# Row sums for a Winograd convolution: two 64-row products, one per half of the columns, in place of one product with a block diagonal table

## The chip, the cores and the metric

The kernel runs on one core of one Trainium2 chip. The metric is the device time of one execution in microseconds. Three runs of the kernel before took 3293.95, 3282.76 and 3287.43 us; the median is 3287.43 us. One further execution was profiled; it took 3285.59 us, and the first to the last instruction in its trace, the span, is 3283.7 us.

## The reference

The input is a batch of 32 images of 56 x 56 places with 96 channels, in float32. Layer 0 is a convolution block, layer 1 a block with a Fourier transform along the tokens and a quantised feed-forward part. Cut to what is computed:

```python
# layer 0
h  = (x - mean(x)) * rsqrt(var(x) + 1e-5) * ln_w + ln_b          # over the 96 channels
x1 = (h @ w_in + b_in)[..., :192]
y  = conv3x3(x1, conv_w, padding="SAME") + conv_b                # 192 -> 96 channels
x  = x + silu(y)
# layer 1, t is x as (32, 3136, 96)
n  = layernorm(t)
h  = relu(bn(n @ w1.T))                                          # 192 channels
X  = fft(h, axis=tokens, norm="ortho")
xr = relu(X.real * rd - X.imag * idg + rb); xi = relu(X.imag * rd + X.real * idg + ib)
t  = t + bn(ifft(xr + 1j * xi).real @ w2.T)
t  = t + quantised_ffn(layernorm(t))                             # 96 -> 384 -> 96
```

The input transform of the convolution is the place of the change. The 3x3 convolution is done as a one-dimensional Winograd scheme along the rows of an image: four output rows come from six sums of input rows, so each of the 14 groups of four rows needs six weighted sums of the rows around it.

## The kernel before

**Layout.** A token of an image is row r and column c of 56 x 56. With `N1 = 112` partitions and `N2 = 28` columns per partition, partition 2r + h holds the 28 columns of half h of row r. All token stages work on tiles of 112 partitions.

**The stage that changes.** An image comes in four chunks of columns, `LN_CHUNKS` (8, 8, 8 and 4 of the 28). `fetch` (L335) loads a chunk `xl` from the input by a DMA on SP's queue. `take_in` (L343) calls `stats` (L120), which takes the sums over the channels on VectorE, the variance on VectorE (L131) and its power of -1/2 on GpSimd (L133), and then scales the chunk on VectorE into one of two buffers `xa` (L349), whose 97th channel is a constant one. `make_image` (L351) calls `image` (L144), which does one TensorE product for each column place j of a chunk. The stationary operand is `xa[:, j, :]`, 112 rows by 97 channels, and the moving one is the table `rows6_sb`, 112 rows by 168 columns. The table has 2 x 6 x 14 columns: for each half h, each of the six sums k and each of the 14 groups g. Since partition 2r + h belongs to half h, an entry is other than zero only where the row's half is the column's half; this is the block diagonal table. So one product yields for 97 channels all 84 sums of both halves. Up to three products share one PSUM tile of tag `q`, and one ScalarE copy (L149) puts them into the image buffer `img`.

**What follows.** `conv` (L151) multiplies `img` with the transformed weights `wv` in 18 products per chunk, on PSUM tiles of the same tag `q`, which has two buffers of one bank each. `to_tokens` (L188) transposes the result, again on tag `q`. The Fourier stages, the products with `w1` and `w2` and the feed-forward part follow with PSUM tiles of other tags.

**Products in float32.** Each float32 product shows as two weight loads and two matmuls in the trace[...]. 28 places x 32 images are 896 products of L148 and 1792 records of each kind.

**Order of the work.** `plan` gives every step of every image a place on a time axis of eight units per image, `order.sort` merges the images, and `run` issues the steps in that order. So the convolution of an image stands beside the Fourier part of the image before it. The program is then put in its final order on each engine by a scheduler that works on an estimated timeline, so neighbouring instructions on TensorE come from several stages. In `plan`, `make_image` stands at up to three places for each chunk, three column places at a time (L500 to L504): 11 steps per image.

## Time and profile before

| | |
|---|---|
| median of three runs | 3287.43 us |
| profiled execution, its own time | 3285.59 us |
| its span, first to last instruction | 3283.7 us |
| TensorE matmul records busy | 3201.2 us, 97% of the span |
| TensorE weight loads busy | 2821.3 us, 86% |
| VectorE busy | 2711.9 us, 83% |
| ScalarE busy | 2319.2 us, 71% |
| GpSimd busy | 586.2 us, 18% |
| mean granted TensorE clock | 0.989 |
| image products (L148) | 1792 matmul records, 324.0 us busy, 308 ns each |
| their copies (L149) | 352, 182.2 us busy in three shapes |
| mean DMA traffic | 108 GB/s |

Busy time of an engine is the time in which at least one of its records runs. [...]the next record may begin before it ends. So the duration of a matmul record is a latency. What a record costs TensorE in a dense stream is the distance from its start to the next start. The trace's timeline merges neighbouring records of one kind into a row with a start and a count; the start of the next row less that of this row, divided by the count, is that distance.

### The profile page before, as it was taken

To read this page: it belongs to the slowest core of one execution; us is meant where nothing else is said; L and a number is where in the kernel's file an instruction comes from. 1 tells how busy PE (TensorE), PEld (TensorE's weight loads), DVE (VectorE), ACT (ScalarE), POOL (GpSimd) and SP (SyncE) were. 2 spreads that over 40 slices of the span, in tenths; PEclk is the share of its full clock that TensorE was granted. 3 is DMA by queue.
4 is the path that set the end of the run, shared out by engine and by line. 5 is a ranking of instruction groups with operands and counts; after the bars stand their busy time and mean duration, and the time that the engine had idled before them with its cause. 6 is when DMAs were issued, how large, how long until landed. Compare 5 with 4: busy or idle time off the path is not lost. (4 is left out here: it accounts for less than half of the span.)

```text
span 3283.7 us, 69648 instructions
## 1 busy us (share of the span) xinstructions
PE 3201.2 (97%) x24597; PEld 2821.3 (86%) x24597; DVE 2711.9 (83%) x8306; ACT 2319.2 (71%) x5616; POOL 586.2 (18%) x397
## 2 busy tenths in 40 slices
PE   6999999999999999999999999999999999999987
PEld 5888888888888888888888888888888888888875
DVE  5568888888888888888888888888888888887887
ACT  2567777777777777777777776777777777777676
POOL 2111112111112111112111112111112111111111
PEclk9999999999999999999999999999999999999997
DMA  4343344433344433344433344433344333443331
GB/s 109 102 110 104 96 114 121 118 105 108 92 121 123 118 102 106 98 119 121 117 106 100 104 121 117 118 97 103 107 121 123 106 108 94 116 121 104 98 108 55
DMA packets 330839, 355.61 MB, mean 108 GB/s; under 512 B 125577, under 2 KB 283673, under 8 KB 330265
## 3 DMA queue, kind: packets, MB, share of 16 engines
q1 hardware_dynamic: 328482, 348.99, 38.5%
q8 instruction: 195, 3.19, 0.4%
q10 hardware_dynamic: 2008, 2.17, 0.2%
q14 instruction: 154, 1.25, 0.1%
HBM read 196.92 MB, written 154.14 MB: 107 GB/s over the span
## 5 line engine op out<-in xcount | busy, mean ns | idle before, releaser
L159 PE MATMUL cv<-img,wv 97*96 97x224 f32 (+1 forms) x4608 | 863.8, 330 | 6.2 <-DVE wv L607 5.4
L159 PEld LDWEIGHTS cv<-img,wv 97*96 97x96 f32 x4608 | 675.1, 163 | 88.1 <-issue 7.1
L133 POOL TENSOR_TENSOR rs_c<-var_c,mhalf 112x8 f32<-112x8 f32 (+1 forms) x128 | 194.1, 1517 | 1900.5 <-DVE var_a L131 994.0
L222 PEld LDWEIGHTS px<-fb_sb,at 112*96 112x96 f32 x3584 | 399.7, 164 | 87.7 <-issue 30.6
L222 PE MATMUL px<-fb_sb,at 112*96 112x112 f32 (+1 forms) x3584 | 429.8, 261 | 20.6 <-DMA at<-da 17.4
L254 PEld LDWEIGHTS pg<-w2a,gt 96*112 96x112 f32 (+1 forms) x3584 | 394.2, 179 | 33.4 <-DVE gt L246 2.9
L254 PE MATMUL pg<-w2a,gt 96*112 96x96 f32 (+1 forms) x3584 | 403.9, 262 | 1.4 <-DVE gt L246 0.6
L226 ACT ACTIVATE av<-px,par_sb 96x224 f32<-96x224 f32 (+1 forms) x448 | 200.1, 447 | 267.8 <-PE px L222 263.4
L284 ACT CAST h<-pf 128x448 f16<-128x448 f32 x672 | 362.5, 539 | 25.2 <-PE pf L282 22.2
L204 PE MATMUL ph<-w1a,n2t 97*112 97x192 f32 x1792 | 369.0, 328 | 1.5 <-ACT n2t L197 1.2
L213 PE MATMUL pa<-h,fa_sb 112*112 112x384 f32 x896 | 366.3, 491 | 0.1
L207 ACT ACTIVATE h<-ph,rs_b 112x192 f32<-112x192 f32 x896 | 330.3, 426 | 29.3 <-PE ph L204 27.9
L148 PE MATMUL im<-rows_sb,xa 112*97 112x168 f32 x1792 | 324.0, 308 | 11.3 <-DVE xa L349 9.6
L133 POOL TENSOR_TENSOR rs_b<-var_b,mhalf 112x8 f32<-112x8 f32 (+1 forms) x128 | 191.7, 1498 | 748.1 <-DVE var_b L131 423.9
L204 PEld LDWEIGHTS ph<-w1a,n2t 97*112 97x112 f32 x1792 | 286.8, 177 | 39.5 <-ACT n2t L197 1.8
L292 DVE TENSOR_SCALAR h<-h,b1q 128x448 f16<-128x448 f16 x658 | 214.2, 326 | 112.0 <-ACT h L284 110.7
L459 DVE TENSOR_SCALAR xn<-t,st_c,rs_c 112x96 f32<-112x96 f32 x896 | 240.0, 320 | 75.4 <-POOL rs_c L133 75.3
L148 PEld LDWEIGHTS im<-rows_sb,xa 112*97 112x97 f32 x1792 | 263.9, 165 | 35.0 <-issue 10.3
L214 ACT COPY u<-pa 112x384 f32<-112x384 f32 x448 | 216.5, 483 | 101.3 <-PE pa L213 97.4
L293 DVE CAST hq<-h 128x448 fp8e5<-128x448 f16 x672 | 257.2, 383 | 12.7 <-ACT h L290 5.9
L237 DVE SCALAR_TENSOR_TENSOR sv<-px,par_sb,av 96x224 f32<-96x224 f32 (+1 forms) x448 | 197.4, 441 | 70.9 <-ACT av L228 66.1
L282 PE MATMUL pf<-n3t,w1q 96*128 96x448 fp8e5 x672 | 242.2, 360 | 8.8 <-ACT h L284 7.6
(110 smaller groups left out, 6022.9 us busy)
## 6 DMA issues: line engine op xcount, KB each, us to landing
da<-u SPq DMA_DIRECT2D x224, 336.0 KB, 3.2
at<-da SPq DMA_DIRECT2D x224, 336.0 KB, 3.8
de<-es SPq DMA_DIRECT2D x224, 168.0 KB, 2.3
y<-de SPq DMA_DIRECT2D x224, 168.0 KB, 2.8
out<-o SPq DMA_DIRECT2D x224, 168.0 KB, 2.2
xl<-in_x SPq DMA_DIRECT2D x96, 336.0 KB, 3.9
x<-in_x SPq DMA_DIRECT2D x96, 336.0 KB, 3.2
xl<-in_x SPq DMA_DIRECT2D x32, 168.0 KB, 2.3
```

The source lines that it names most:

```text
L133: nc.gpsimd.tensor_tensor(rs, var, mhalf[:, :n], ALU.pow)
L148: nc.tensor.matmul(ps[:, j], xa[:, j, :], rows6_sb, start=True, stop=True)
L159: nc.tensor.matmul(ps[:, at], wv[:, k, dx, :], cols, start=(dx == 0), stop=(dx == 2))
L204: nc.tensor.matmul(ph[:, j, :], n2t[:, 2 * j2 + j, :], w1a, start=True, stop=True)
L207: nc.scalar.activation(h[:, j], ph[:, j], AF.Relu, scale=rs[:, 2 * j2 + j : 2 * j2 + j + 1])
L213: nc.tensor.matmul(pa, fa_sb, h, start=True, stop=True)
L222: nc.tensor.matmul(px[:, j], at[:, j, i * C : (i + 1) * C], fb_sb[:, first(p) : first(p + 1)], start=True, stop=True)
L254: nc.tensor.matmul(pg[:, j, :], lhs, w2a[:, i, :], start=(i == 0), stop=(i == 1))
L282: nc.tensor.matmul(pf, w1q[:, k * 128 : (k + 1) * 128], n3t, start=True, stop=True)
L284: nc.scalar.copy(h1, pf)
L293: nc.vector.tensor_copy(hq[:, k, :], h2, saturate=False)
L459: nc.vector.tensor_scalar(xc[:, j], im.t[i][:, at, :C], mu[:, at : at + 1], rs[:, at : at + 1], ALU.subtract, ALU.mult)
```

## The change

The image stage takes its input from a second copy of the input, `xh`, laid out in advance by the host program: for each image, 128 rows of 28 columns, of which rows 0 to 55 are the left halves of the image rows, rows 64 to 119 are the right halves, and rows 56 to 63 and 120 to 127 are zeros. `fetch` loads 128 partitions of it. `stats`, the scaling and the buffers `xa` have 128 partitions in this stage; the rest of the kernel keeps 112.

The table `rows6_sb` has the 84 sums once for partitions 0 to 63 and once for 64 to 127. `image` does two products for each column place: rows 0 to 63 with the left half, rows 64 to 127 with the right half, each with a moving operand of 64 rows by 84 columns. The products of the two halves go to two PSUM tiles of tag `q`, up to four column places in each, and two ScalarE copies put them into `img`. `plan` has seven steps of four column places per image where it had 11 of up to three.

```diff
     def image(xa, n, b, j0):
-        ps = psq.tile([C + 1, n, 2, WC * WG], F32, tag="q", name=f"im_{b}_{j0}")
+        ps = [psq.tile([C + 1, n, WC * WG], F32, tag="q", name=f"im_{b}_{j0}_{h}") for h in range(2)]
         for j in range(n):
-            nc.tensor.matmul(ps[:, j], xa[:, j, :], rows6_sb, start=True, stop=True)
-        nc.scalar.copy(img[:, :, j0 + 1 : j0 + 1 + n].rearrange("c h j k g -> c j h (k g)"), ps)
+            for h in range(2):
+                rows = slice(64 * h, 64 * h + 64)
+                nc.tensor.matmul(ps[h][:, j], xa[rows, j, :], rows6_sb[rows], start=True, stop=True)
+        for h in range(2):
+            nc.scalar.copy(img[:, h, j0 + 1 : j0 + 1 + n].rearrange("c j k g -> c j (k g)"), ps[h])
...
-    rows6_sb = const.tile([N1, 2 * WC * WG], F32, name="rows6_sb")
+    rows6_sb = const.tile([128, WC * WG], F32, name="rows6_sb")
-    xas = [const.tile([N1, 8, C + 1], F32, name=f"xa{i}") for i in range(2)]
+    xas = [const.tile([128, 8, C + 1], F32, name=f"xa{i}") for i in range(2)]
...
-        im.xl[i] = xnp.tile([N1, j1 - j0, C], F32, tag=tag, bufs=bufs, name=f"xl_{im.b}_{i}")
-        nc.sync.dma_start(im.xl[i], im.tokens[:, j0:j1, :])
+        im.xl[i] = xnp.tile([128, j1 - j0, C], F32, tag=tag, bufs=bufs, name=f"xl_{im.b}_{i}")
+        nc.sync.dma_start(im.xl[i], xh[im.b, :, j0:j1, :])
...
-            ats = (-0.95, -0.7) if last else (0.2, 0.5, 0.85) if i == 2 else (0.25, 1.0, 1.5)
+            ats = (-0.95,) if last else (0.2, 0.85) if i == 2 else (0.25, 1.25)
...
-            for part, j in enumerate(range(0, j1 - j0, 3)):
-                put(at + ats[part], make_image, i, j, min(3, j1 - j0 - j))
+            for part, j in enumerate(range(0, j1 - j0, 4)):
+                put(at + ats[part], make_image, i, j, 4)
...
-    rows6 = np.zeros((HW, 2, 2, WC, WG))
+    rows6 = np.zeros((2, 64, WC, WG))
...
-                for h in range(2):
-                    rows6[r, h, h, :, g] = sums[:, i]
+                rows6[:, r, :, g] = sums[:, i]
...
+def half_columns(x):
+    xh = np.zeros((x.shape[0], 2, 64, N2, C), x.dtype)
+    xh[:, :, :HW] = x.reshape(-1, HW, 2, N2, C).transpose(0, 2, 1, 3, 4)
+    return xh.reshape(-1, 128, N2, C)
```

## The prediction

> **What bounds the kernel now.** I read the engine totals first, then the split into stages, then TensorE's timeline, because a matmul record's duration is a latency and tells little of what it costs.

> The split into four stretches gives busy time by engine, then the granted clock and the DMA share:

> ```profile
> core 0: us, PE busy (x) PEld busy (x) DVE busy (x) ACT busy (x) POOL busy (x), PEclk, DMA share, GB/s
> 0.00:100.00 100.00, 72.98 (x419) 61.85 (x420) 51.40 (x178) 31.71 (x65) 20.84 (x26) 0.93 0.42 110
> 100.00:3000.00 2900.00, 2876.24 (x22281) 2553.06 (x22280) 2430.69 (x7411) 2087.90 (x5074) 527.85 (x349) 1.00 0.40 110
> ```

> From 100 to 3000 us TensorE is without a running matmul for 24 us in 2900, at full clock, while ScalarE is busy 72% and the DMA engines 40%. So the span follows TensorE's stream nearly one to one, and 1652 of the 1792 image records lie in this stretch. The waits agree: ScalarE waits for the image products 42.9 us, TensorE for the copies 0.8 us.

> Next comes what a record costs. Two pieces of TensorE's timeline (start, duration, what, count):

> ```profile
> 1507.67 1.02 PE L148 MATMUL im<-rows_sb,xa 112*97 112x168 f32 x6
> 1508.52 2.44 PE L159 MATMUL cv<-img,wv 97*96 97x224 f32 x12
> ...
> 1500.22 0.94 PE L263 MATMUL pe<-gw,ib_sb 112*112 112x96 f32 x8
> 1501.00 0.78 PE L299 MATMUL po<-w2q,hq 128*112 128x96 fp8e5 x12
> ...
> 1519.80 0.87 PE L148 MATMUL im<-rows_sb,xa 112*97 112x168 f32 x5
> 1520.51 1.55 PE L254 MATMUL pg<-w2a,gt 96*114 96x96 f32 x14
> 1521.90 0.82 PE L271 MATMUL py<-y,ia_sb 113*112 113x384 f32 x2
> ...
> 20.75 0.85 PE L597 MATMUL ps_we<-cw,wt 96*97 96x96 f32 x8
> 21.43 1.59 PE L148 MATMUL im<-rows_sb,xa 112*97 112x168 f32 x10
> ```

> Start to start: an image record takes (1508.52 - 1507.67) / 6 = 142 ns, and again 0.71 / 5 = 142. It has 168 moving columns, so 0.84 ns a column: it is bound by the stream. The convolution record has 224 columns and the same rate, 189 ns. Records with 96 moving columns would take 81 ns at that rate, but the products of L263 (112 weight columns) take 0.78 / 8 = 98 and those of L254 here (114 weight columns) 1.39 / 14 = 99. These are bound by the weight load, at 98 / 112 = 0.87 ns per weight column. L597, with 97 weight columns as the image products have, takes 0.68 / 8 = 85 ns, which is 97 x 0.87. So a record of a float32 product (not of a transpose[...]) costs the larger of 0.84 x moving columns and 0.87 x weight columns. Rows do not enter: L254 loads 96 rows, L263 112.

> [...] The kernel before has one product in another mode, the setup's L647 with one weight column[...]:

> ```profile
> 42.01 0.25 PE L644 MATMUL ps_w<-ident,w2s 96*96 96x96 f32 x1
> 42.01 0.09 PEld L647 LDWEIGHTS ps_o<-ident,o 96*1 96x1 f32 x1
> 42.09 0.24 PE L647 MATMUL ps_o<-ident,o 96*1 96x96 f32 x1
> 42.10 0.81 PEld L159 LDWEIGHTS cv<-img,wv 97*96 97x96 f32 x5
> 42.18 0.92 PE L159 MATMUL cv<-img,wv 97*96 97x224 f32 x4
> ```

> L647 starts 80 ns after L644, and the next product in the full mode 90 ns after L647 while L647 is still running for 150 ns. No drain shows on either side. It is one case, of columns and not of rows.

> **The change part by part.**

> *TensorE.* Removed are 1792 records at 142 ns, 254.5 us. Added are 1792 products, thus 3584 records, of 84 moving and 97 weight columns. The stream of one is 84 x 0.84 = 71 ns, the load 85 ns; the load decides. 3584 x 85 = 304.6 us. Balance: +50 us. The moving columns halve, but each half loads all 97 channels anew, and the load was hidden behind 168 columns before and is no longer hidden behind 84.

> *Side by side.* The two halves might overlap. The code alternates them, but the scheduler doesn't keep that: in the changed program's order on TensorE, 1792 image products stand in 468 unbroken runs, most often four of one half and later four of the other, with products of other stages between. Only at 252 places does one half follow the other directly; 1072 times it is the same half. If at each of the 252 a product of two records hid wholly beside its neighbour, it would save 252 x 170 = 43 us; one record each, 21 us; if loads go one after another, nothing. As the load is the bound and I see one load stream, I take 0, with 0 to 43 as bounds.

> *Change of mode.* 468 runs are entered and left, 936 changes. From L647 I take 0 ns each. Upper bound: an image record lasts 306 ns (median) and its successor starts after 142, so a full drain exposes 164 ns; with the next load exposed too, 249 ns.

> *ScalarE.* Before, 224 copies of 504 columns at 580 ns, 96 of 336 at 434 and 32 of 168 at 328, together 182 us. After, 448 of 336 columns at 434, 194 us. The 12 us lie on an engine that is idle for 812 us in the long stretch, hidden behind TensorE. Without that cover they would be 0.4%.

> *PSUM.* An image step holds both `q` buffers, and there are 33 tiles of that tag per image where there were 30. The next user waits for the copy of the tile two before it. That needs about 0.9 us: 0.3 of matmul latency, 0.43 of copy, 0.2 of queueing as my allowance. Laying the spacings above along both orders, I find some 20 places of about 1000 in each with less than 1 us of TensorE work between, 5 us short in all against 4. I take 0, at most 10 us if ScalarE's queue, where copies stand behind other stages' work, is late.

> *Edits with one answer.* `xl` grows from 112 to 128 partitions: 96 loads of 336 KB and 32 of 168 KB become 384 and 192, 5 MB more on 356, issued 2.5 of the plan's units (about 31 us) ahead and landing in 3.9; the count and order of SP's issues stay. VectorE's and GpSimd's instructions keep their lengths per partition (948, 350, 160 ns; 1790 ns). The padding rows are zeros with a zero table. All cost 0, behind TensorE; if the loads came late, VectorE's sums would (they wait 87 us for `xl` now), then `xa`, then the image products.

> *Order elsewhere.* The scheduler reorders neighbours throughout. The 24 us of gaps in the long stretch limit what a better order gives; a worse one may cost as much. I take 0 +- 15.

> Sum: the profiled execution's 3285.6 us (span 3283.7 and 1.9 around it) + 50 = 3336. The median of the runs is 1.8 us above that execution, so 3337 us, +1.5%. A difference under 0.3%, 10 us, could not be told from none.

> **The rivals.**

> *Drain* (20%): each of 936 changes exposes 164 ns, 154 us, so 3491 us; with loads exposed, 936 x 249 = 233 us and 3570. For it: [...]that a change of rows may cost what a change of columns doesn't. Against: L647.

> *Partial overlap* (13%): halves that meet save one record each, 21 us: 3316 us. [...]Against: only 252 meetings, and a load-bound stream.

> *Short loads* (15%): a load into half the rows takes less than the stream. Place: each of the 3584 records; break-even is 254.5 us / 3584 = 71 ns, which is exactly the stream of 84 columns. So shorter loads alone give 3287 us, no change. Together with matmuls of the two halves that overlap where they meet, the mean falls below 71 ns and the kernel is faster: 252 x 142 = 36 us at most, 3251. [...]Against: 96 and 112 rows load alike.

> *Nothing on TensorE's path* is excluded by the 24 us of gaps.

> **How the numbers follow.** Load-bound and no drain 52% (own range 3320 to 3355, from the +-15 of the order); drain 20%, partial overlap 13%, short loads 15%, of which 10% end faster and 5% the same. Slower: 52 + 20 + 13 = 85%. The range for 8 in 10 reaches from 3280, which takes in the short loads without overlap, to 3500, which takes in the simple drain; left out are the faster case and the drain with exposed loads, 10% and 7%.

> **What would show it.** Right: 3584 image records with starts 85 ns apart within a run, in either half; a next start 85 to 100 ns after a run's last image record; about 15 us more per ten images in the long stretch; ScalarE's copies at 434 ns. Drain: a jump of some 160 ns at each run's first and last record. Overlap: starts a few ns apart where halves meet. Short loads: 71 ns apart in a run. Wrong altogether would be a TensorE that idles over 3% in the long stretch, waiting for ScalarE's copies or for `xa`.

## The result

The changed kernel takes 3443.91 us (median of 4 runs, 3440.47 to 3451.86) against 3288.9 us (the three runs known before, and a fourth): a ratio of 1.0469, 95% interval 1.0449 to 1.0488. It is 155 us slower. I had forecast slower by 50 us, with 3337 us; the sign and the range held, the size did not. The profiled execution has a span of 3439.5 us against 3283.7.

The split by stages, long stretch of the changed kernel (busy time of TensorE, its loads, VectorE, ScalarE, GpSimd; clock; DMA share):

```profile
core 0: us, PE busy (x) PEld busy (x) DVE busy (x) ACT busy (x) POOL busy (x), PEclk, DMA share, GB/s
100.00:3000.00 2900.00, 2884.30 (x22740) 2469.19 (x22739) 2317.67 (x7038) 2015.87 (x4907) 507.44 (x333) 1.00 0.38 107
```

TensorE is without a running matmul for 16 us where it was 24. It is still the engine that sets the time, at full clock, and it has more to do. The image stage in the table of groups (busy time and mean length of one, then idle time before it):

```profile
L151 PEld LDWEIGHTS im<-rows_sb,xa 64*97 64x97 f32 x3584 | 316.9, 165 | 114.6 <-issue 42.7
...
L151 PE MATMUL im<-rows_sb,xa 64*97 64x84 f32 x3584 | 389.7, 261 | 9.3 <-DVE xa L353 8.8
...
L153 ACT COPY img<-im 97x336 f32<-97x336 f32 x448 | 191.3, 444 | 91.9 <-PE im L151 88.8
```

The counts are the forecast ones, and the copies are near their price (444 ns for 434). The image products waited for `xa`, and so for the larger loads behind it, no longer than before: 8.8 us, once, at the start, where it was 9.6. But the image records are busy 389.7 us against 324.0, and the time went up by more than that difference. The rest shows only in TensorE's timeline, which has the answer to the pieces shown of before (start, duration, what, count):

```profile
1501.48 0.82 PE L217 MATMUL pa<-h,fa_sb 112*112 112x384 f32 x2
1502.24 0.91 PE L151 MATMUL im<-rows_sb,xa 64*97 64x84 f32 x8
1503.08 0.90 PE L208 MATMUL ph<-w1a,n2t 97*112 97x192 f32 x4
1503.91 0.91 PE L151 MATMUL im<-rows_sb,xa 64*97 64x84 f32 x8
1504.76 0.82 PE L303 MATMUL po<-w2q,hq 128*112 128x96 fp8e5 x12
```

and the same product of L208 in the kernel before, where it is L204:

```profile
1506.82 0.81 PE L204 MATMUL ph<-w1a,n2t 97*112 97x192 f32 x4
1507.47 0.35 PE L282 MATMUL pf<-n3t,w1q 96*128 96x448 fp8e5 x1
```

Eight image records take 1503.08 - 1502.24 = 0.84 us where 8 x 86 ns are 0.69. The four records of L208 between the two runs take 0.83 us; in the kernel before four of them took 0.65 (1506.82 to 1507.47). The two of L217 before the first run take 0.76, for 0.65. So both the runs and their neighbours are longer. I call an unbroken row of image records a run of records, and the distance to the next start that a record of a form has in a dense stream its price. Record by record, the medians over the changed kernel's runs are: the record before a run is 93 ns longer than its price; the first image record is 151 ns from the second where alone in a stream it is 86; the last one is 176 ns from its successor; and that successor is typically 77 ns longer than its price. That is 93 + 65 + 90 + 77 = 325 ns for each run of records.

The start of such a run, TensorE's matmuls and loads side by side:

```profile
1518.02 0.35 PE L286 MATMUL pf<-n3t,w1q 96*128 96x448 fp8e5 x1
...
1518.30 1.17 PEld L151 LDWEIGHTS im<-rows_sb,xa 64*97 64x97 f32 x16 [0.34 <-ACT img L153]
1518.30 1.33 PE L151 MATMUL im<-rows_sb,xa 64*97 64x84 f32 x16
...
1519.56 0.27 PEld L141 LDWEIGHTS tp_n<-ident,xn 112*96 112x96 f32 x3
1519.56 0.40 PE L141 MATMUL tp_n<-ident,xn 112*96 112x112 f32 x2
```

The record of L286 costs 192 ns in a dense stream; here the next starts 0.28 us after it. The first image load appears only with the first image matmul, and the first load of L141 only with its first matmul. In the kernel before, the load of L159 at 42.10 us began 80 ns ahead of its own matmul. This holds throughout. Matched load by matmul, an image load inside a run begins 72 ns ahead of its matmul (median); the first load of a run and the first load after a run begin 2 ns ahead, in nine of ten runs between 1 and 4. In the kernel before, the first image load of a run was 160 ns ahead. By the mode of a product I mean its shape where the times show a change: 64 rows here (64 weight columns or one, in runs below), against 96 to 128 rows and weight columns in the products around. So at a change of mode no load was pulled ahead, and on the way in there was a pause of 93 ns. I call this pause a drain. The record of L286 lasts 0.35 us and the next starts after 0.28, 70 ns before its end. So it is at the changes into and out of the runs, whatever the record before (median 70 ns on either side; on the way in, nine of ten lie between 69 and 71). That is what a wait for the record before would look like, if it is done 70 ns before the end that the trace draws; the wait itself no trace shows. The copy that the view names as releaser is not the cause, as it ended at 1518.14, 0.16 us before the load began.

**The account.** From the starts in each trace I took every record's distance to the next start and compared it with the price of its form in a dense stream. Image part: the price of the image records, what they took beyond it, the excess of the record just before a run, and that of the record just after a run's last. Standing still: all excesses over 250 ns. It is more than the 24 or 16 us without a running matmul above, since a record counts as running for a while after the next could have started, and since the end of the program is in it. From 100 us on, in us:

| kernel | median, one run marked * | image part | standing still |
|---|---|---|---|
| before | 3288.9 | 240 | 72 |
| changed | 3443.9 | 406 | 55 |
| e1_full_height | 3354.0 | 295 | 79 |
| e2_half_rows | 3407.9 | 369 | 54 |
| e4_half_columns | 3385.8* | 357 | 56 |
| e3_alternate | 3344.7 | 214 | 125 |
| e10_first_free | 3352.0 | 215 | 133 |
| e5_in_blocks | 3381.3 | 299 | 91 |
| e8_no_priority | 3383.0 | 248 | 134 |
| e7_six_places | 3380.6 | 212 | 150 |
| e7b_six_places | 3408.8 | 211 | 176 |
| e6_two_places | 3605.2* | 300 | 200 |
| e11_one_half | 3242.9 | 150 | 114 |

For the changed kernel against the one before: the price of the records +48.5 us, the way in +42.5, within the runs +45, the way out +30, standing still -17.5; with +6 of other work that ran in the first 100 us before and now comes later, and +1 of small waits, 156 us, which is the difference of the spans. The split is good to about 5 us: with another rounding of the prices some of it moves from "within the runs" to "the price".

### The profile page after: what moved, and what is told of

It reads as the page before. It is cut to its first block, busy times and chain, and to the rows that moved or that the text cites. A ratio compares the mean times of both kernels' runs of the same rounds, so it can differ in the third digit from the quotient of the medians.

```text
span 3439.5 us, 73409 instructions
## 1 busy us (share of the span) xinstructions
PE 3370.2 (98%) x26389; PEld 2875.6 (84%) x26389; DVE 2724.8 (79%) x8306; ACT 2354.9 (68%) x5712; POOL 588.6 (17%) x397
## 4 chain that ended last, share of the span: by engine, by line
PE 91%; DMA 5%; DVE 2%; ACT 2%; issue 1%; POOL 0%; ACTq 0%; SPq 0%; DVEq 0%; POOLq 0%
PE cv L163 21%; PE px L226 10%; PE pg L258 10%; PE im L151 9%; PE ph L208 9%; PE pa L217 8%; PE tp_n L141 5%; PE pe L267 5%; PE py L275 4%; PE po L303 4%; PE pf L286 3%; PE st L195 2%; DMA at<-da 2%; DMA da<-u 1%; DMA de<-es 1%; DMA ib_sb<-in_ib 1%
## 5 line engine op out<-in xcount | busy, mean ns | idle before, releaser
L163 PE MATMUL cv<-img,wv 97*96 97x224 f32 (+1 forms) x4608 | 880.8, 330 | 1.1 <-DVE sd L175 1.1
L226 PE MATMUL px<-fb_sb,at 112*96 112x112 f32 (+1 forms) x3584 | 441.3, 263 | 17.3 <-DMA at<-da 12.9
L151 PEld LDWEIGHTS im<-rows_sb,xa 64*97 64x97 f32 x3584 | 316.9, 165 | 114.6 <-issue 42.7
L151 PE MATMUL im<-rows_sb,xa 64*97 64x84 f32 x3584 | 389.7, 261 | 9.3 <-DVE xa L353 8.8
L208 PE MATMUL ph<-w1a,n2t 97*112 97x192 f32 x1792 | 380.1, 331 | 0.0
L217 PE MATMUL pa<-h,fa_sb 112*112 112x384 f32 x896 | 369.9, 495 | 0.8 <-ACT h L211 0.8
L208 PEld LDWEIGHTS ph<-w1a,n2t 97*112 97x112 f32 x1792 | 286.1, 177 | 56.2 <-issue 4.5
L463 DVE TENSOR_SCALAR xn<-t,st_c,rs_c 112x96 f32<-112x96 f32 x896 | 230.6, 322 | 54.0 <-POOL rs_c L133 54.0
L153 ACT COPY img<-im 97x336 f32<-97x336 f32 x448 | 191.3, 444 | 91.9 <-PE im L151 88.8
L286 PE MATMUL pf<-n3t,w1q 96*128 96x448 fp8e5 x672 | 241.9, 360 | 9.6 <-ACT h L288 8.7
```

Of the source, the lines that this page charges most:

```text
L151: nc.tensor.matmul(ps[h][:, j], xa[rows, j, :], rows6_sb[rows], start=True, stop=True)
L163: nc.tensor.matmul(ps[:, at], wv[:, k, dx, :], cols, start=(dx == 0), stop=(dx == 2))
L208: nc.tensor.matmul(ph[:, j, :], n2t[:, 2 * j2 + j, :], w1a, start=True, stop=True)
L217: nc.tensor.matmul(pa, fa_sb, h, start=True, stop=True)
L226: nc.tensor.matmul(px[:, j], at[:, j, i * C : (i + 1) * C], fb_sb[:, first(p) : first(p + 1)], start=True, stop=True)
L286: nc.tensor.matmul(pf, w1q[:, k * 128 : (k + 1) * 128], n3t, start=True, stop=True)
```

## The experiments

The theory was "load and mode": twice the weight loads, no longer hidden, and 325 to 340 ns for each unbroken run of image products in the mode of 64 rows. The rival, "steps and tiles": the seven steps, the second PSUM tile, the 448 copies and the new order.

**e1_full_height: the loads without the mode.** The kernel before, its input without padding, with the changed kernel's steps, tiles and copies. The product, shown against that of the changed kernel:

```diff
-                nc.tensor.matmul(ps[h][:, j], xa[rows, j, :], rows6_sb[rows], start=True, stop=True)
+                nc.tensor.matmul(ps[h][:, j], xa[:, j, :], rows6_sb[:, 84 * h : 84 * h + 84], start=True, stop=True)
```

> Two products per column place with 84 moving columns, seven steps of four places, two PSUM tiles and two copies as in the changed kernel, but each product over all 112 rows (one half of the block diagonal table), so TensorE never changes its mode. Theory 'load and mode': only the load is left of the change, 3584 records at 86 ns against 1792 at 142, +54 us, so about 3343 us, with starts 86 ns apart and no jump at the ends of a run. Rival 'steps and tiles' (the PSUM tiles, the copies and the new order cost the time): it stays near the changed kernel, about 3440 us.

Measured: 3353.95 us against 3289.04, ratio 1.0198 (1.0181 to 1.0215), +65 us. TensorE's timeline:

```profile
1512.73 0.84 PE L149 MATMUL im<-rows_sb,xa 112*97 112x84 f32 x8
1513.41 0.96 PE L265 MATMUL pe<-gw,ib_sb 112*112 112x96 f32 x8
```

Eight records in 0.68 us, 85 ns each, and no jump. The image part is 55 us over that of the kernel before, the standing still 7 us. So the steps, tiles and copies with the doubled loads make 65 us of the 155, most of it loads. The rival had 3440 us here and falls. The other 90 go with what this kernel leaves out: the mode, and the padded second copy of the input. e2_half_rows takes the mode alone.

**e2_half_rows and e4_half_columns: the mode without the loads.** The kernel before, first with rows 0 to 63 alone, then with 64 channels alone (the lines of two edits, each with its name behind it).

```diff
-            nc.tensor.matmul(ps[:, j], xa[:, j, :], rows6_sb, start=True, stop=True)
+            nc.tensor.matmul(ps[:, j], xa[:64, j, :], rows6_sb[:64], start=True, stop=True)      # e2_half_rows
+            nc.tensor.matmul(ps[:64, j], xa[:, j, :64], rows6_sb, start=True, stop=True)         # e4_half_columns
```

> The kernel before with its image products over rows 0 to 63 only (the sums of rows 64 to 111 are left out): the same 1792 records of 168 columns, bound by the stream, the same steps and tiles, but in the mode of 64 rows, in 397 unbroken runs. Theory 'load and mode': each run pays on the way in (93 ns, and a first load in the open, 80 ns) and on the way out (90 ns and 77 ns), 340 ns in all; 397 x 340 = 135 us, so about 3424 us. Rival 'steps and tiles', and my prediction's price of 0 for a change: 3289 us.

> The kernel before with its image products for 64 of the 97 channels only (the other channels are left out and the image buffer holds zeros for them): 1792 records of 168 columns [...]in 396 runs. If a change of the column mode is free, as the one product of the setup suggested to me: 3289 us, starts 142 ns apart and no jump at the ends of a run. If any change of mode drains: about 93 + 56 + 90 + 77 = 316 ns a run, +125 us, about 3414 us.

Measured: e2_half_rows 3407.88 us, ratio 1.0367 (1.0351 to 1.0382), +119 us; e4_half_columns 3385.81 us in its one run, +97 us. TensorE's timeline of e2_half_rows:

```profile
1501.21 0.82 PE L213 MATMUL pa<-h,fa_sb 112*112 112x384 f32 x2
1501.96 0.52 PE L148 MATMUL im<-rows_sb,xa 64*97 64x168 f32 x2
1502.42 0.36 PE L282 MATMUL pf<-n3t,w1q 96*128 96x448 fp8e5 x1
```

The two image records take 0.46 us where two in a full-height stream take 0.28, and the two before them 0.75 for 0.65. Medians: 93 ns before a run, the first record at 221 and the last at 233 ns for 142, 77 ns after. That is 93 + 79 + 91 + 77 = 340 ns, as expected; 397 runs of them are 135 us, and the image part grew by 129. TensorE stood still 18 us less, and the time grew by 119, 16 less than expected. The steps, tiles, copies and the input are those of the kernel before, so none of them is needed for the 340 ns. In the column mode the figures are 93, 193, 236 and 77, and the image part grew by 117 (125 expected). Here a change of columns cost what a change of rows cost, but for a first load in the open of 51 ns and not 79. At 0.87 ns a column (98 ns for 112, in the kernel before), 64 columns for 97 would make a difference of 29 ns; these are 28.

**e9_plain_product: why I had seen none.** The setup's one product with a single weight column was a transposing one.

```diff
-        nc.tensor.transpose(ps[:1, :C], o2, ident[:C, :C])
+        nc.tensor.matmul(ps[:1, :C], o2, ident[:C, :C], start=True, stop=True)
```

> The kernel before with the setup's one product in a narrow tile[...] made a plain product and not a transposing one. In the kernel before it began 84 ns after its predecessor and its successor 82 ns after it. If transposing products keep the full mode whatever their tile, and that is why I saw no drain there: now jumps of some 90 ns on the way in and on the way out, and the time as before, 3289 us. If a tile of one column is free of the drain: no jump.

Measured: 3296.7 us in one run, no different. TensorE's timeline:

```profile
42.79 0.37 PE L644 MATMUL ps_w<-ident,w2s 96*96 96x96 f32 x1
43.09 0.48 PE L647 MATMUL ps_o<-ident,o 96*1 96x96 f32 x2
43.50 1.44 PE L159 MATMUL cv<-img,wv 97*96 97x224 f32 x3
```

Now L647 begins 0.30 us after L644 and its successor some 0.29 us after its last record. In the kernel before it was 84 and 82 ns. The clock was about half here, by my estimate: the records of L159 lie 373 ns apart for 189, and in the kernel before they lie 353 ns apart where 0.53 of the clock was granted (37 to 42 us). That would explain twice the 82 to 84 ns, some 165, and leave 130 on either side. Two signs do not rest on the clock. The loads of L647 and of the L159 after it begin 2 ns ahead of their matmuls, where it was 84 and 80 in the kernel before. And on both sides the next record starts 70 ns before the drawn end of the one before, where it was 162. Both are the marks of the changes of mode above. With the same shape, the transposing product had neither. This is one place in one run.

**e3_alternate and e5_in_blocks: side by side.** The changed kernel with the eight products of a step held together in the order of TensorE, alternating or in two blocks.

```diff
+        prev = None
+        nc.vector.memset(ps[1][:, :1, :1], 0.0)
+        with tc.high_priority():
             for j in range(n):
                 for h in range(2):          # e5_in_blocks: the two loops exchanged
...
-                    nc.tensor.matmul(ps[h][:, j], xa[rows, j, :], rows6_sb[rows], start=True, stop=True)
+                    at = nc.tensor.matmul(ps[h][:, j], xa[rows, j, :], rows6_sb[rows], start=True, stop=True)
+                    if prev is not None:
+                        tc.add_manual_dep(at.ins, prev.ins.name, NOSYNC, reason="image")
+                    prev = at
```

> The changed kernel with its eight image products of a step held together and alternating between the halves (an order edge from each to the next, priority, and one tiny VectorE fill of the second tile so that both tiles are there before the first product): 225 runs in place of 468. Theory 'load and mode' with halves side by side: 16 records pay 8 x 86 ns and some 340 ns for the two changes, 1030 ns against 1136 before, so 224 x -106 ns = -24 us, about 3265 us, starts in pairs 6 and 80 ns apart. If halves do not run side by side when alternating: 16 x 86 + 340 = 1716 ns, +130 us, 3419 us. Rival 'steps and tiles': no faster than the changed kernel, 3444 us or, with both tiles held longer, more.

> As e3_alternate in all but the order within a step: four products of one half and then the four of the other, still held together (222 runs). It tells side by side from number of runs. In the changed kernel such unbroken runs of 16 records took 1390 ns where alternating ones took 1030, since the halves overlap only around the middle. So 218 x 360 ns = 78 us over e3_alternate's 3345 us: about 3423 us. If the alternation gives nothing and only the number of runs counts: 3345 us.

Measured: e3_alternate 3344.66 us, ratio 1.0175 (1.016 to 1.019); e5_in_blocks 3381.27 us, ratio 1.0264 (1.0247 to 1.0282). TensorE's timelines, e3_alternate first:

```profile
1513.24 0.92 PE L155 MATMUL im<-rows_sb,xa 64*97 64x84 f32 x16
1514.09 0.90 PE L282 MATMUL py<-y,ia_sb 113*112 113x384 f32 x2
```

and e5_in_blocks:

```profile
1524.79 1.33 PE L155 MATMUL im<-rows_sb,xa 64*97 64x84 f32 x16
1526.04 0.62 PE L233 MATMUL px<-fb_sb,at 112*96 112x112 f32 x4
```

Sixteen records take 0.85 us alternating and 1.25 us in blocks, for 1.38 at 86 ns each. Alternating starts come in pairs, 6 and 80 ns apart: the second half is free, loads included, and a record costs 43 ns. So the idea of the change works on TensorE: the image part of e3_alternate is 26 us below the kernel before (24 expected). Between e3_alternate and e5_in_blocks the image part differs by 85 us (78 expected), but the time by only 37.

Where e3_alternate missed is the rest. The time should have been 3265 us. TensorE stood still 125 us where it had stood still 72, and waited more often for the fetch that opens the second half of the Fourier part. The group of that fetch's users in e3_alternate:

```profile
L233 PE MATMUL px<-fb_sb,at 112*96 112x112 f32 (+1 forms) x3584 | 440.2, 264 | 45.4 <-DMA at<-da 28.5 <-PE im L155 7.7 <-issue 3.6
```

and in the kernel before:

```profile
L222 PE MATMUL px<-fb_sb,at 112*96 112x112 f32 (+1 forms) x3584 | 429.8, 261 | 20.6 <-DMA at<-da 17.4 <-DVE sv L240 2.2 <-ACT h L207 0.6
```

The idle time before these products doubled. Waits under 250 ns grew by some 15 us, too. Some 10 us more come at the start: the first convolution begins at 48 us, not 38. That is so in the changed kernel as well, so it is no price of holding products together.

**e8_no_priority, e10_first_free, e7_six_places, e7b_six_places, e6_two_places: looking for the gain, and the size of a step.** All are e3_alternate with a part altered (the fence has lines of all of them, with names behind): without the raised priority; with the first image, in the setup, left free; with six column places a step (in e7_six_places the fourth step overwrote places that a convolution of the image before still had to read, so sums of two images mix; e7b_six_places has it later and leaves the first image free); with two places a step.

```diff
-        with tc.high_priority():                                         # e8_no_priority: loop without it
...
-        nc.vector.memset(ps[1][:, :1, :1], 0.0)
+        if b: nc.vector.memset(ps[1][:, :1, :1], 0.0)                     # e10_first_free, e7b_six_places; edges too
...
-            for part, j in enumerate(range(0, j1 - j0, 4)):
-                put(at + ats[part], make_image, i, j, 4)
...
+        for j, when in zip(range(0, N2, 6), (-5.75, -3.75, -2.5, -1.2, -0.95)):   # e7b_six_places
+            put(CONV + when, make_image, j, min(j + 6, N2))
...
+            for part, j in enumerate(range(0, j1 - j0, 2)):               # e6_two_places
+                put(at + ats[part], make_image, i, j, 2)
```

> As e3_alternate with the order edges and the fill, but without the raised priority of the image products: 320 runs, 161 of them of a whole step. Image runs: 896 x 0.172 + 320 x 0.344 = 264 us, 32 us over e3_alternate. If the raised priority is what made TensorE wait for loads of the Fourier part in e3_alternate (75 us more standing still in all than before): about 3345 + 32 - 75 = 3302 us. If the waits come with the two tiles held at once: about 3377 us.

> As e3_alternate, but the first image, whose steps run in the setup, is left as in the changed kernel (no order edges, no fill). e3_alternate began its first convolution 10 us later than the kernel before. If that is all that this part costs: 10 us off, about 3335 us. Image runs as in e3_alternate.

> As e3_alternate with six column places a step (five steps an image, over the borders of the chunks), so 188 runs in place of 225. At 172 ns for a place and 344 ns for a run's two changes: 896 x 0.172 + 188 x 0.344 = 219 us for the image runs, against 232 us with e3_alternate's 225 and 259 us before. With e3_alternate's idle time elsewhere about 3330 us; with no more idle time than the kernel before about 3250 us, faster than before. If the price of a run is not fixed but per product, no gain over e3_alternate.

> Six column places a step with the fourth step of an image put after the convolution that reads the places it overwrites, and the first image left free: 159 runs. Image runs 896 x 0.172 + 159 x 0.344 = 209 us, 50 us under the kernel before. If TensorE's work alone decided: 3240 us. If another limit lies near 3340 us, as e3_alternate and e8_no_priority suggest, whose TensorE work is under the kernel before and whose time is over it: 3330 to 3370 us.

> As e3_alternate with two column places a step, so 411 unbroken runs in place of 225: only the number of mode changes grows. At 344 ns a run: +64 us of TensorE's image runs, spread as drains of about 93 ns at each end and first loads in the open. The whole time moves by less where TensorE stood still before: e5_in_blocks put 85 us on TensorE and moved the time by 37. So 3345 + 30 to 64 = 3375 to 3409 us. If the number of changes does not matter: 3345 us.

Measured: 3382.99 us (ratio 1.0275, 1.0254 to 1.0295), 3351.96 (1.0189, 1.016 to 1.0218), 3380.58 (1.0261, 1.024 to 1.0282), 3408.77 (1.0357, 1.0339 to 1.0375) and, in one run, 3605.19 us. None beats the kernel before. The image part moves with the number of runs: with 159 runs it is 211 us (209 expected), with 320 it is 248 (264 expected), with 411 it is 300, 86 over e3_alternate's (64 expected). The last is no clean measure of the price, as the mean granted clock of e6_two_places falls to 0.950 from 0.989. The whole time does not follow. e7b_six_places has 3 us less image work than e3_alternate and takes 64 us more, with 51 us more standing still; it and e6_two_places lie above every figure that I had expected. The raised priority is not what made TensorE wait: without it, it stands still 134 us, and the time is near the 3377 us that I had set for waits that come with holding two tiles at once. Leaving the first image free gained nothing. In e6_two_places TensorE is idle for 39.5 us before image products until an image copy ends. The wait for the fetch is 65.7 us in e7b_six_places and 56.9 in e6_two_places, but 25.3 in e7_six_places, which stands still for 150, so no single wait explains them all. I suppose that holding products together takes away work with which TensorE would fill its waits; that is not shown, and what gives way in each of these orders I did not separate.

**e11_one_half: what a quicker stage could bring.** The kernel before with one half's products alone.

```diff
-            nc.tensor.matmul(ps[:, j], xa[:, j, :], rows6_sb, start=True, stop=True)
+            nc.tensor.matmul(ps[:, j, 0], xa[:, j, :], rows6_sb[:, :84], start=True, stop=True)
```

> The kernel before with image products of the left half's 84 columns only (the right half's sums are left out, the left half's are copied in their place): 1792 full-height records at 86 ns in place of 142, -100 us of TensorE work, no change of mode, the steps, tiles and copies of the kernel before. It asks what a quicker image stage could bring at all. If TensorE's stream sets the time down to there: 3189 us. If another limit lies close below the kernel before: not under about 3250 us, with TensorE standing still in between.

Measured: 3242.94 us, ratio 0.9858 (0.9843 to 0.9873), -45 us for some 90 us less image work. Its group of the fetch's users:

```profile
L225 PE MATMUL px<-fb_sb,at 112*96 112x112 f32 (+1 forms) x3584 | 431.8, 262 | 49.1 <-DMA at<-da 44.2 <-DVE sv L243 2.7 <-ACT h L210 1.5
```

The wait for the fetch grows from 17.4 to 44.2 us with nothing held together. Once per image all tiles of one stage must have been stored before the first of the next can be fetched, and here TensorE got there sooner and waited longer. Work added to TensorE showed almost fully in the time (119 of 129 us in e2_half_rows); the work taken away here showed by half.

## Why the prediction was wrong

**The bound: right.** TensorE's stream set the time before and after, and the forecast's reading, a distance between starts and not a duration, is what found the cause. "Nearly one to one" held for added work, 119 of 129 us; for work taken away, e11_one_half has 45 of 90. I had not thought of the two directions apart.

**Twice the loads: right.** 85 ns forecast, 86 measured, +50 us forecast, +48.5 in the account; e1_full_height has 85 ns with full-height products. As said, rows did not enter: records of 64 rows were 86 ns apart (changed kernel), those of 112 rows 85 (e1_full_height). The rival "short loads" is out, as it needed 71 ns.

**The change of mode: this step failed.** "From L647 I take 0 ns each." Measured were 325 ns for a run in the changed kernel, 340 in e2_half_rows, and the drains, open loads and ends of the 468 runs come to some 142 us: 42.5 on the way in, 30 on the way out and 69 within the runs (45 net, and the 24 that overlapping gave back, below). No trace of before showed a change of mode by a plain product. The 164 ns of the rival were my estimate, a record's 306 ns less the 142 to its successor, and I set them aside for one example that could not speak: L647 is a transpose, as its line in the code says, with its successor 82 ns after it. In e9_plain_product the same product, not transposing, had the next start 70 ns before its drawn end, as at the other changes. I noted the transposes as another kind where I set up the price of a record, and did not ask whether they are another kind here. The rival "drain" had the price, 2 x 164 = 328 ns a run against 325, but by luck: 164 was the distance to the drawn end of the record, and the next one starts 70 ns before that end. So it is some 93 of drain, and 65 to 77 of a load in the open make up the rest. Its 3491 us are 47 too many, mostly because it had no overlap and no standing still to give back. The forecast range held the result only because it reached to 3500 for this rival.

**Side by side: 0 was too low; it gave back some 24 us.** "As the load is the bound and I see one load stream" was the error. In e3_alternate products of the two halves start 6 ns apart, and the loads keep up, with 43 ns a record for 86. In the changed kernel, between 100 and 3150 us, 316 image records start within 22 ns of their predecessor instead of 86: 209 x 80 ns and 107 x 71. The rival "partial overlap" had 21 us for this.

**Order and gaps: just outside the +-15.** Standing still fell by 17.5 us: as TensorE takes longer, it waits less. **ScalarE and PSUM: 0 was right to some 10 us.** e1_full_height has them together with the weight loads: 65 us, of which the image part is 55, so at most some 10 us are left for them, the order and the start. **Padding and larger transfers: no run has them alone.** The account leaves no room for more than a few us, and the image products waited for `xa` no longer than before. The lengths held: on VectorE 952, 350 and 163 ns at 128 partitions for 948, 350 and 160 at 112, on GpSimd 1706 ns for 1790 (changed kernel and kernel before).

In sum 48.5 + 142 - 24 - 17.5 + 7 is 156 us. The forecast had 50; the price of the mode, which turned out the largest term, stood in it at 0.

## What to carry to other kernels

A product of half height was not half a product here. As the data are the weights, each half loads all its 97 columns anew, and against a stream of 84 columns, 71 ns by the 0.84 ns a column of before, the load decided: 86 ns a record. By an estimate from these runs, the two halves would have paid on TensorE only if their products followed each other directly and long enough to earn the change of mode: some 340 ns a run (e2_half_rows) against 112 ns gained for each column place (284 - 172, two records at 142 in the kernel before and four at 43 in e3_alternate), so over three places a run. The scheduler, left free, made 230 of the 468 runs only eight records long. And the image part is not the time: e3_alternate took 26 us off the one and added 56 to the other. Before a cost is put at 0 on one row of a trace, check that the row is of the same kind of instruction; a transpose was not.
